# A graph network on one core: an addition moved between stages, and the order of GpSimd's and VectorE's work inside a layer-0 tile

## The chip, the cores and the metric

The kernel runs on one core of one Trainium2 chip. The metric is device time in microseconds, lower is better. A core has four engines that compute: TensorE (PE in the profile; its weight loads, which overlap the matmuls, are listed as PEld), VectorE (DVE), ScalarE (ACT) and GpSimd (POOL). SyncE (SP) issues most of the transfers. Each engine runs its own instructions in the order in which they were written for it, and waits on semaphores for the other engines. Operands lie in SBUF, 128 partitions wide; TensorE writes its sums to PSUM, and the other engines fetch them from there ("evict" them).

## The reference, cut to what matters

`x` is (8, 2048, 64): B = 8 samples, N = 2048 nodes, C = 64 features. `adj` is a 2048 x 2048 matrix whose rows are 0/1 patterns divided by their sums. Each of two layers applies `adj` twice, mixes the results by weights, adds the layer's input and normalizes over the features.

```python
def _L0_gnn_ref(x, A, embedding, weight, bias):
    w = jnp.einsum('nd,dkio->nkio', embedding, weight)     # one weight matrix per node, D = 16
    b = jnp.einsum('nd,do->no', embedding, bias)
    As = [jnp.eye(N, dtype=x.dtype), A]
    As.append(2.0 * (A @ As[-1]) - As[-2])                 # K = 3
    x_g = jnp.einsum('knm,bmc->bnkc', jnp.stack(As, 0), x)
    return jnp.einsum('bnki,nkio->bno', x_g, w) + b

# layer 1: x_stack = [x0] + 2 x [A x0, 2 A (A x0) - x0], then
    out = jnp.einsum('bnf,fo->bno', x_cat, weight) + bias

x = _layernorm(x + _L0_gnn_ref(x, adj, L0_gnn_embedding, L0_gnn_weight, L0_gnn_bias), axis=-1)
x = _layernorm(x + _L1_gnn_ref(x, adj, adj, L1_gnn_weight, L1_gnn_bias), axis=-1)
```

## The kernel before

The 2048 nodes are 16 tiles (NT) of 128 (P). Numbers of fp32 are split in a high and a low half (in layer 0 also a mixed one), so that TensorE can multiply them in the fp32r form; the splitting is most of the work of VectorE and ScalarE. The row factor 1/sum is kept apart from the 0/1 pattern. The stages, one after the other, with their stretches of the span in us:

- 10 to 123: the first hop, `adj` times x (L254).
- 123 to 226: the second hop as seven products of quarter matrices (`seven_products`, L631).
- 226 to 543: layer 0's mixing with the per-node weights, tile by tile (`mix0`, L415), with its normalization.
- 543 to 651: layer 1's first product with `adj`, called the third hop here, again `seven_products`, now with `to=to_zT`.
- 651 to 776: the fourth hop, the last normalization and the stores.

**A tile of layer 0.** TensorE multiplies the tile's operands `tt[k][n]` (k = x itself, its first and its second hop; n = high, low, mixed) by the 16 weight matrices of the embedding, in 8 slots (g, dg): g is a half of the samples, dg a group of 4 of the 16 matrices. Each slot fills one pair of PSUM banks from a pool of four pairs, `pm`, used in turn and by the transposes and projections of the same tile as well. In slots with dg > 0 VectorE takes the four parts of `pm` times the node's embedding value, and adds them into `acc` (L427). In the two slots with dg = 0 ScalarE scales them into `aside` (L425), GpSimd sums these (L430) and adds them to `acc`: for g = 0 ahead of slot (1, 2), for g = 1 at the tile's end (`add_aside`, L399).

The order of the work is written by hand: `ordered` keeps the written order on each engine, and the dictionary `at` says what is put into which slot, ahead of that slot's matmuls and evictions. During tile t there are put in:

- the operands of tile t + 1 (`parts`, L309 to 320). Each of the three generators `of_x`, `of_hop`, `of_second` has two steps: first ScalarE's copy to the high half (L312), then VectorE's low half (L314), ScalarE's scaled copy (L318) and GpSimd's sum of both (L319). `of_hop` takes its source from PSUM, where TensorE transposed it (buffer `pt`).
- the normalization of tile t - 1 (`layernorm`, L358 to 374), as a generator of steps. Ahead of the first step: VectorE's sum s (L361, L362) and GpSimd's subtraction xc (L364), written at the end of tile t - 1. First step: ScalarE's square (L352). Second: VectorE's sum ss (L369), ln_v (L333), ScalarE's root (L335). Third: VectorE's reciprocal and refinement (L338 to 344), GpSimd's product (L373). Before the change they stand in slots (0, 1), (0, 2) and (0, 3).
- GpSimd's product of tile t + 2's second hop with the row factors (`times_r`, L679 to 682), in slot (1, 2), and GpSimd's start of tile t + 1's sum, x plus the node's bias (`begin_sum`, L382 to 391, two instructions), in slot (1, 3).
- the normalized tile's transpose to `hT`, and after the tile the `project`ion of tile t - 1 by layer 1's weights (L434 to 454): for each g, TensorE fills `pu`, ScalarE copies two thirds of it to their places (L451), VectorE copies the last third and adds layer 1's bias `bias1` to it (L452). This third goes to bc(2, t), that is, the part that neither of layer 1's hops is applied to.

`bias1` is the last 64 columns of the tile `pack_sb`, which one transfer loads with the embedding values. That transfer, and those of `bias_sb`, `wl` and `rrow`, stand in the list `loads`, and are issued by SP's queue one at a time: the first in the later part of the first hop, while more than three are left (L507), the others one per step of the second hop (L621). `bias1`'s mean is taken off in `weights` (L184 to 187).

**The third hop.** `run` (L265) goes through the steps (p, kk) of seven products of KK = 8 steps. Each step makes its operands some steps ahead (`y_high` 4, `y_low` 3, `operands` 2) and then issues 8 matmuls in `use`; what stands in the dictionary `more` under (p, kk) is issued right after these. The output of the finished products is taken off PSUM by `put` on VectorE, through `todo`, two entries per step.

Of the kernel before, what the change touches and what calls it, by code (L numbers as in the profile page):

```python
# [9 lines left out]
F32 = mybir.dt.float32  # L10
# [4 lines left out]
ALU = mybir.AluOpType  # L15
# [3 lines left out]
P = 128  # L19
# [20 lines left out]
def pattern(  # L40
# [55 lines left out]
    def bc(s, t):  # L96
        return z[s][t].rearrange("p (b c) -> p b c", c=C)
# [9 lines left out]
    part = keep.tile([P, B], F32, tag="part", name="part")  # L107
    rrow = rowpool.tile([P, N], F32, tag="rrow", name="rrow")
    ident = keep.tile([P, P], F32, tag="ident", name="ident")
    pack_sb = const.tile([P, NT * D + C], F32, tag="pack", name="pack_sb")  # L110
    emb_sb = pack_sb[:, : NT * D].rearrange("p (t d) -> p t d", d=D)
    bias1 = pack_sb[:, NT * D :]
    ebias = const.tile([P, NT, C], F32, tag="ebias", name="ebias")


# [11 lines left out]
    def ordered(ins):  # L127
        if in_order:
            tc.keep_in_program_order(ins)
# [32 lines left out]
    wl = work2.tile([P, 5, C], F32, tag="t0", name="wl")  # L162
    bias_sb = work2.tile([P, N // 4 + C], F32, tag="t0", name="bias_sb")

    loads = [(bias_sb, bias), (pack_sb, pack[:, : NT * D + C]), (wl.rearrange("p k o -> p (k o)"), pack[:, NT * D + C :])]
    loads += [(rrow, diag.to_broadcast([P, N]))]

    def weights():

# [264 lines left out]
    def project(t, hT, pus=None):  # L434


        for g in range(2):
            pm = bank("pu") if pus is None else pus[g]
            for i in range(2):
                for j in range(2):  # L440
                    q = slice(j * C, (j + 1) * C)
                    nc.tensor.matmul(
                        pm[:, j, i * 3 * C : (i + 1) * 3 * C], lhsT=hT[q, 2 * g + i, :], rhs=v[q],
                        start=True, stop=True,
                    )
            got = pm[:, :, : 6 * C].rearrange("p j (i k c) -> p j i k c", i=2, k=3)

            order = ["p (i j) c -> p j i c", "p (j i) c -> p j i c", "p (j i) c -> p j i c"]
            to = [bc(k, t)[:, 4 * g : 4 * g + 4, :].rearrange(order[k], j=2) for k in range(3)]
            for k in range(2):  # L450
                ordered(nc.scalar.copy(to[k], got[:, :, :, 2 - k, :]))  # L451
            ordered(nc.vector.tensor_tensor(  # L452
                to[2], got[:, :, :, 0, :], bias1.unsqueeze(1).unsqueeze(1).to_broadcast([P, 2, 2, C]), ALU.add,
            ))


    HALF = N // 2
# [26 lines left out]
    def hop_x(g, kk, j):  # L484
        k = kk + KK * j

        def features(got):
            if g == 0 and k == 0:
                got["raws"] = [load_slab(adj[h, 0, :, :Q], [P, Q]) for h in range(2)]

        def operands(got):
            if g == 0 and k == 0:

                s = got["s"] = spool.tile([P, 2, Q], F32R, tag="s", name="s")
                hl = got["hl"] = [hpool.tile([P, B * C], F32R, tag="hl", name="hl") for _ in range(2)]
                high(z[0][0], hl)
                for h in range(2):
                    ordered(nc.vector.tensor_scalar(s[:, h], got["raws"][h], 0.0, None, ALU.not_equal))
                    if h == 0:
                        low(z[0][0], hl)  # L500
            else:
                if g == 0:
                    load(nc.sync, z[0][k], x[k].rearrange("n b c -> n (b c)"))
                raw = load_slab(adj[:, k, :, g * Q : (g + 1) * Q].rearrange("h m n -> m h n"), [P, 2, Q])
                got["s"] = places(raw)
                got["hl"] = halves(z[0][k])
                if g == 1 and len(loads) > 3:  # L507
                    load(nc.sync, *loads.pop(0))
            couple.append(got["s"])
            if j == 1:  # L510
                put_together(g, kk, *couple)
                couple.clear()

        def out(i):
            t = 4 * g + i if i < 4 else 4 * g + i + 4
            a, r = accs[i], rcol[:, t : t + 1]
            if i % 2:
                ordered(nc.vector.tensor_scalar_mul(z[1][t], a, r))
            else:
                ordered(nc.scalar.activation(z[1][t], a, AF.Copy, scale=r))  # L520

        def use(got):
            s, hl = got["s"], got["hl"]
            if kk == 0 and j == 0:
                accs[:] = banks(8)
            last = kk == KK - 1 and j == 1
            add_block(accs, s.rearrange("p h n -> p (h n)"), hl, kk == 0 and j == 0, last)
            if last:
                for i in range(8 if g == 0 else 4):
                    out(i)  # L530
            seen = xcpool.tile([P, 2, Q], BF16, tag="ln_xc", name="seen")
            i = g * NT + k
            ordered(nc.scalar.activation(seen, s, AF.Copy, accum_out=nonzero[:, i : i + 1]))
            if j == 1:
                ordered(nc.scalar.dma_start(out=quarters[kk, :, :, g, :], in_=seen))
            else:
                ordered(nc.scalar.dma_start(out=corner[kk, :, g, :], in_=seen[:, 0]))
            if last and g == 1:
                stores.pop(0)()

                todo.extend(lambda i=i: out(i) for i in range(4, 8))

        return [(4, features), (2, operands), (0, use)]


# [244 lines left out]
    def quarter_back(a, b, which):  # L790
        ts, got = range(8 * a, 8 * a + 8), []

        def two(n):
            for m in (n, n + 1):
                add_back(ts[m], got[m], b)

        work_here = [nothing, nothing, lambda: got.extend(back(ts, sums3[which], b)), nothing]
        return work_here + [lambda n=n: two(n) for n in range(0, 8, 2)]

    third = seven_products(0, to_zT, sums3, {  # L800
        (0, 5): [last_transposed],
        (0, 6): [last_projected],
        3: quarter_back(1, 1, 1), 4: quarter_back(0, 1, 0), 5: quarter_back(0, 0, 1),
    }, wait=2)

# [11 lines left out]
    for t in range(NT):  # L817
# [3 lines left out]
        if not last:  # L821
            got["tt"], of_x, of_hop, of_second = operands(t + 1)
            of_hop = of_hop()
            at[0, 2] += [lambda it=of_hop: next(it), lambda it=of_hop: next(it)]
            at[0, 3] += [lambda it=of_x: next(it)]
            at[1, 0] += [lambda it=of_x: next(it)]
            at[1, 1] += [lambda it=of_second: next(it)]
            at[1, 2] += [lambda it=of_second: next(it)]
            if t + 2 < NT:
                at[1, 2] += [lambda: times_r(t + 2)]  # L830
            at[1, 3] += [lambda: got.update(acc=begin_sum(t + 1))]
        if t > 0:
            at[0, 1] += [lambda: next(norm)]
            at[0, 2] += [lambda: next(norm)]
            at[0, 3].insert(0, lambda: next(norm))
            at[1, 2 if last else 3] += [lambda: got.update(hT=transpose(h, "hT"))]
        if last:
            at[0, 1] += [lambda: early(0)]
# [491 lines left out]
```

## Time and profile before

| what | us |
|---|---|
| median of 3 runs (lowest, highest) | 778.22 (777.99, 778.36) |
| the profiled execution's own time | 778.42 |
| its span | 776.6 |

The span runs from the first to the last recorded instruction of that execution, so 1.8 us of its time lie around it. Busy time by stage (us):

| stretch of the span | length | PE | DVE | ACT | POOL |
|---|---|---|---|---|---|
| first hop, 10 to 123 | 113.0 | 113.0 | 86.2 | 57.9 | 0 |
| second hop, 123 to 226 | 103.0 | 103.0 | 72.5 | 72.9 | 4.4 |
| layer 0, 226 to 543 | 317.0 | 310.7 | 274.3 | 147.3 | 217.1 |
| third hop, products 0 and 1, 543 to 573 | 30.0 | 30.0 | 20.0 | 24.6 | 2.9 |
| third hop, products 2 and 3, 573 to 603 | 30.0 | 30.0 | 17.2 | 22.7 | 0 |
| third hop, the rest, 603 to 651 | 48.0 | 48.0 | 29.7 | 32.2 | 0 |
| fourth hop, 651 to 776 | 125.0 | 119.0 | 82.6 | 19.8 | 24.8 |

The granted TensorE clock was 0.998 of full speed over the span. A tile of layer 0 takes about 19.8 us.

How to read the lines shown below. A line of the engine shares has the busy time of an engine, its share of the span and its number of instructions. A line of the waits view reads: engine, what it was about to write and its line in the code, the releaser it waited for, then us in total, times, longest. A line of a timeline has the start in us, the duration (of a run of several, from the first's start to the last's end), the engine, the line, the operation, out<-in with partitions x elements, and in brackets how long the engine had waited for what. "L427" is line 427 of the kernel.

### The profile page before, as it was taken

The numbers are of one execution on the slowest core, as the hardware profiler recorded it, in microseconds if no ns is written. First come the engines' busy times: TensorE is split into PE (matmuls) and PEld (weight loads), VectorE is DVE, ScalarE is ACT, GpSimd is POOL, SyncE is SP. The second block draws the span as 40 slices with busy tenths as digits, with TensorE's granted clock in tenths as the row PEclk, the third lists the DMA queues.
The fourth block names the chain that finished last, engine by engine and source line by source line (L and its number), as shares of the span: only waits on it lengthen the run. The fifth ranks groups of instructions, "written<-read, shape, count | busy, mean of one in ns | idle before, by whom it ended". The sixth has DMA issues, their size and how long they took to land.

```text
span 776.6 us, 17970 instructions
## 1 busy us (share of the span) xinstructions
PE 762.1 (98%) x7246; PEld 675.4 (87%) x7246; DVE 585.3 (75%) x1246; ACT 380.4 (49%) x720; POOL 249.9 (32%) x245
## 2 busy tenths in 40 slices
PE   9999999999999999999999999999999999999996
PEld 6888888888889999999999999999888888888885
DVE  6779766678648888888888888888765657768653
ACT  4446443878753444444444444445787664112111
POOL 0000000000036777777777777774100000012341
PEclk9999999999999999999999999999999999999999
DMA  8998995545410000000000000001444344565631
GB/s 309 384 383 294 335 322 173 188 156 170 163 42 16 17 16 16 15 16 16 16 16 16 16 15 16 2 29 43 142 158 148 137 149 144 170 189 158 215 130 45
DMA packets 73403, 96.77 MB, mean 125 GB/s; under 512 B 4704, under 2 KB 48224, under 8 KB 73184
## 3 DMA queue, kind: packets, MB, share of 16 engines
q1 hardware_dynamic: 61904, 76.66, 30.4%
q10 hardware_dynamic: 11408, 18.89, 6.5%
q8 instruction: 59, 0.97, 0.5%
q14 instruction: 32, 0.26, 0.1%
HBM read 76.65 MB, written 18.87 MB: 123 GB/s over the span
## 4 chain that ended last, share of the span: by engine, by line
PE 60%; DVE 25%; POOL 6%; issue 5%; ACT 2%; DMA 1%; SPq 0%; DVEq 0%; POOLq 0%
PE accT L631 26%; DVE acc L427 16%; PE acc L254 15%; PE a L254 9%; PE accT L254 6%; DVE parts L314 3%; PE pm L415 2%; POOL xc L364 2%; POOL acc L399 2%; DVE ln_v L333 2%; DVE s L361 1%; POOL acc L386 1%; DVE ss L369 1%; ACT sq L352 1%; DMA raw<-in_adj 1%
## 5 line engine op out<-in xcount | busy, mean ns | idle before, releaser
L415 PE MATMUL pm<-wh,hl 64*128 64x256 f32 x1536 | 239.9, 286 | 5.5 <-DVE acc L427 5.5
L415 PE MATMUL pm<-wm,parts 64*128 64x256 f32 x1536 | 235.0, 280 | 0.0
L415 PE MATMUL pm<-wl,parts 64*128 64x256 f32 x1536 | 234.9, 280 | 0.0
L631 PE MATMUL accT<-s,hl 128*128 128x512 f32 x896 | 205.7, 390 | 0.0
L631 PEld LDWEIGHTS accT<-s,hl 128*128 128x128 f32 x896 | 167.5, 188 | 35.4 <-issue 0.2
L427 DVE SCALAR_TENSOR_TENSOR acc<-pm,pack_sb,acc 128x256 f32<-128x256 f32 x384 | 185.1, 482 | 15.7 <-PE pm L415 3.8
L415 PEld LDWEIGHTS pm<-wh,hl 64*128 64x128 f32 x1536 | 164.4, 188 | 10.2 <-DVE acc L427 9.2
L415 PEld LDWEIGHTS pm<-wl,parts 64*128 64x128 f32 x1536 | 164.4, 188 | 0.0
L415 PEld LDWEIGHTS pm<-wm,parts 64*128 64x128 f32 x1536 | 164.2, 187 | 0.0
L619 ACT CAST s<-raw 128x1024 fp32r<-128x1024 bf16 x104 | 109.2, 1050 | 39.7 <-ACT hl L234 25.4
L254 PE MATMUL acc<-hl,s 128*128 128x512 f32 x512 | 117.5, 391 | 0.3 <-DVE s L223 0.2
L254 PEld LDWEIGHTS acc<-hl,s 128*128 128x128 f32 x512 | 95.7, 188 | 21.7 <-DVE hl L238 0.7
L682 POOL TENSOR_TENSOR z<-z,rrow 128x512 f32<-128x512 f32 x16 | 21.0, 1314 | 212.9 <-DVE z L655 212.9
L425 ACT ACTIVATE aside<-pm,pack_sb 128x256 f32<-128x256 f32 x128 | 50.2, 475 | 66.0 <-PE pm L415 66.0
L234 ACT CAST hl<-z 128x256 fp32r<-128x256 f32 (+1 forms) x96 | 47.5, 511 | 65.6 <-PE acc L254 24.9
L430 POOL TENSOR_TENSOR aside<-aside 128x512 f32<-128x512 f32 x64 | 69.7, 1090 | 14.8 <-ACT aside L425 12.2
L254 PE MATMUL a<-hl,s 128*128 128x512 f32 (+1 forms) x352 | 73.4, 370 | 0.0
L254 PEld LDWEIGHTS a<-hl,s 128*128 128x128 f32 x352 | 61.9, 188 | 11.3
L319 POOL TENSOR_TENSOR parts<-parts 128x512 fp32r<-128x512 f32 x45 | 57.8, 1285 | 27.8 <-DVE parts L314 27.1
L238 DVE TENSOR_TENSOR hl<-z,hl 128x512 fp32r<-128x512 f32 (+1 forms) x96 | 53.3, 563 | 16.2 <-ACT hl L234 13.5
L287 POOL TENSOR_TENSOR z<-z,got 128x512 f32<-128x512 f32 x3 | 4.8, 1625 | 143.4 <-ACT got L286 143.4
L254 PE MATMUL accT<-hl,s 128*128 128x512 f32 x192 | 44.3, 390 | 0.0
(130 smaller groups left out, 815.3 us busy)
## 6 DMA issues: line engine op xcount, KB each, us to landing
raw<-in_adj SPq DMA_DIRECT2D x59, 512.0 KB, 5.8
raw<-sums_of SPq DMA_DIRECT2D x64, 256.0 KB, 2.7
sums_of<-z ACTq DMA_DIRECT2D x16, 512.0 KB, 5.9
raw<-quarters SPq DMA_DIRECT2D x32, 256.0 KB, 2.7
raw<-in_adj SPq DMA_DIRECT2D x16, 384.0 KB, 3.0
quarters<-seen ACTq DMA_DIRECT2D x16, 256.0 KB, 5.8
xt<-in_xT SPq DMA_DIRECT2D x16, 256.0 KB, 2.6
z<-in_x SPq DMA_DIRECT2D x15, 256.0 KB, 6.8
```

The costliest lines, as they stand in the source:

```text
L234: ordered(nc.scalar.copy(to[0], src))
L238: ordered(nc.vector.tensor_tensor(to[1], src, to[0], ALU.subtract))
L254: nc.tensor.matmul(accs[i], lhsT=s[:, i * P : (i + 1) * P], rhs=hl[h], start=(first and h == 0), stop=(last and h == 1),)
L314: ordered(nc.vector.tensor_tensor(view(low), src, view(high), ALU.subtract))
L319: ordered(nc.gpsimd.tensor_tensor(mixed, mixed, low, ALU.add))
L415: nc.tensor.matmul(pm[:, j, i], lhsT=tt[k][n][q, 2 * g + i, :], rhs=w_parts[n][k][q, ds, :], start=(k == 0 and n == 0), stop=(k == 2 and n ...
L425: ordered(nc.scalar.activation(aside[g][:, d], got, AF.Copy, scale=e))
L427: ordered(nc.vector.scalar_tensor_tensor(part, got, e, part, ALU.mult, ALU.add))
L430: ordered(nc.gpsimd.tensor_tensor(aside[g][:, :n], aside[g][:, :n], aside[g][:, n : 2 * n], ALU.add))
L619: ordered(nc.scalar.copy(s, got["raw"]))
L631: nc.tensor.matmul(acc[i][:, c], lhsT=hl[h][:, i * P : (i + 1) * P], rhs=S[:, c * 512 : (c + 1) * 512], start=(kk == 0 and h == 0), stop=( ...
L682: ordered(nc.gpsimd.tensor_tensor(to, to, r, ALU.mult))
```

## The change

There are three parts.

1. `bias1` becomes a tile of its own with a transfer of its own (one entry more in `loads`, and the bound in L507 goes from 3 to 4). `project` copies all three thirds on ScalarE, without the bias. The bias is added later by a new function `add_bias(t)`, one VectorE instruction of 128x512 per tile, in the steps of products 2 and 3 of the third hop.
2. `times_r(t + 2)` moves from slot (1, 2) to slot (0, 2), and `begin_sum(t + 1)` from slot (1, 3) to slot (0, 3) (behind the normalization's product L373 and the high half of x).
3. For all tiles but the last, the normalization's square (L352) is written in slot (0, 2) between the high half of the hop and its low half, where before it stood a slot earlier, ahead of both. In the last tile, which prepares no next one, the second and third steps of the normalization move one slot forward, to (0, 1) and (0, 2).

```diff
--- before.py
+++ after.py
@@ -107,9 +107,9 @@
     part = keep.tile([P, B], F32, tag="part", name="part")
     rrow = rowpool.tile([P, N], F32, tag="rrow", name="rrow")
     ident = keep.tile([P, P], F32, tag="ident", name="ident")
-    pack_sb = const.tile([P, NT * D + C], F32, tag="pack", name="pack_sb")
+    pack_sb = const.tile([P, NT * D], F32, tag="pack", name="pack_sb")
     emb_sb = pack_sb[:, : NT * D].rearrange("p (t d) -> p t d", d=D)
-    bias1 = pack_sb[:, NT * D :]
+    bias1 = keep.tile([P, C], F32, tag="bias1", name="bias1")
     ebias = const.tile([P, NT, C], F32, tag="ebias", name="ebias")
 
 
@@ -162,8 +162,8 @@
     wl = work2.tile([P, 5, C], F32, tag="t0", name="wl")
     bias_sb = work2.tile([P, N // 4 + C], F32, tag="t0", name="bias_sb")
 
-    loads = [(bias_sb, bias), (pack_sb, pack[:, : NT * D + C]), (wl.rearrange("p k o -> p (k o)"), pack[:, NT * D + C :])]
-    loads += [(rrow, diag.to_broadcast([P, N]))]
+    loads = [(bias_sb, bias), (pack_sb, pack[:, : NT * D]), (wl.rearrange("p k o -> p (k o)"), pack[:, NT * D + C :])]
+    loads += [(bias1, pack[:, NT * D : NT * D + C]), (rrow, diag.to_broadcast([P, N]))]
 
     def weights():
 
@@ -447,11 +447,12 @@
 
             order = ["p (i j) c -> p j i c", "p (j i) c -> p j i c", "p (j i) c -> p j i c"]
             to = [bc(k, t)[:, 4 * g : 4 * g + 4, :].rearrange(order[k], j=2) for k in range(3)]
-            for k in range(2):
+            for k in range(3):
                 ordered(nc.scalar.copy(to[k], got[:, :, :, 2 - k, :]))
-            ordered(nc.vector.tensor_tensor(
-                to[2], got[:, :, :, 0, :], bias1.unsqueeze(1).unsqueeze(1).to_broadcast([P, 2, 2, C]), ALU.add,
-            ))
+
+    def add_bias(t):
+        to = bc(2, t)
+        ordered(nc.vector.tensor_tensor(to, to, bias1.unsqueeze(1).to_broadcast([P, B, C]), ALU.add))
 
 
     HALF = N // 2
@@ -504,7 +505,7 @@
                 raw = load_slab(adj[:, k, :, g * Q : (g + 1) * Q].rearrange("h m n -> m h n"), [P, 2, Q])
                 got["s"] = places(raw)
                 got["hl"] = halves(z[0][k])
-                if g == 1 and len(loads) > 3:
+                if g == 1 and len(loads) > 4:
                     load(nc.sync, *loads.pop(0))
             couple.append(got["s"])
             if j == 1:
@@ -800,6 +801,7 @@
     third = seven_products(0, to_zT, sums3, {
         (0, 5): [last_transposed],
         (0, 6): [last_projected],
+        **{(2 + t // KK, t % KK): [lambda t=t: add_bias(t)] for t in range(NT)},
         3: quarter_back(1, 1, 1), 4: quarter_back(0, 1, 0), 5: quarter_back(0, 0, 1),
     }, wait=2)
 
@@ -821,18 +823,18 @@
         if not last:
             got["tt"], of_x, of_hop, of_second = operands(t + 1)
             of_hop = of_hop()
-            at[0, 2] += [lambda it=of_hop: next(it), lambda it=of_hop: next(it)]
-            at[0, 3] += [lambda it=of_x: next(it)]
+            at[0, 2] += [lambda it=of_hop: next(it), lambda: next(norm) if t else None, lambda it=of_hop: next(it)]
+            if t + 2 < NT:
+                at[0, 2] += [lambda: times_r(t + 2)]
+            at[0, 3] += [lambda it=of_x: next(it), lambda: got.update(acc=begin_sum(t + 1))]
             at[1, 0] += [lambda it=of_x: next(it)]
             at[1, 1] += [lambda it=of_second: next(it)]
             at[1, 2] += [lambda it=of_second: next(it)]
-            if t + 2 < NT:
-                at[1, 2] += [lambda: times_r(t + 2)]
-            at[1, 3] += [lambda: got.update(acc=begin_sum(t + 1))]
         if t > 0:
-            at[0, 1] += [lambda: next(norm)]
-            at[0, 2] += [lambda: next(norm)]
-            at[0, 3].insert(0, lambda: next(norm))
+            if last:
+                at[0, 1] += [lambda: next(norm)]
+            at[0, 1 if last else 2] += [lambda: next(norm)]
+            at[0, 2 if last else 3].insert(0, lambda: next(norm))
             at[1, 2 if last else 3] += [lambda: got.update(hT=transpose(h, "hT"))]
         if last:
             at[0, 1] += [lambda: early(0)]
```

## The prediction

> **What bounds the kernel now.** I read the page's engine shares first, then layer 0 in stretches of one node tile, then who waited for whom there, then the timelines of VectorE and GpSimd over one tile.
>
> ```profile
> PE 762.1 (98%) x7246; PEld 675.4 (87%) x7246; DVE 585.3 (75%) x1246; ACT 380.4 (49%) x720; POOL 249.9 (32%) x245
> ```
>
> TensorE is busy 98% of the span, so all that can be won without touching its matmuls lies in its few gaps. In layer 0 (226 to 545 us) the waits view has these:
>
> ```profile
> DVE s L361 <- POOL acc L399: 16.2, 15, 1.2
> ...
> PEld pm L415 <- DVE acc L427: 9.2, 14, 1.1
> DVE parts L314 <- ACT hl L312: 5.7, 14, 0.4
> ```
>
> Once per tile, fourteen times, TensorE's weight load for the first bank of the next tile waits about 0.6 us for VectorE's evictions L427: it needs the PSUM bank of slot (1, 2). 9.2 us is the most that layer 0 can give. A tile takes this long (columns: stretch, length, then busy time of PE, PEld, DVE, ACT, POOL):
>
> ```profile
> 304.13:323.93 19.80, 19.49 (x320) 19.19 (x320) 17.33 (x37) 9.32 (x23) 14.21 (x15) 1.00 0.05 15
> ```
>
> No engine but TensorE is full, so the order on VectorE and GpSimd decides. The tile that starts at 304.13, VectorE's timeline and then GpSimd's:
>
> ```profile
> 308.84 2.04 DVE L427 SCALAR_TENSOR_TENSOR acc<-pm,pack_sb,acc 128x256 f32<-128x256 f32 x4
> 311.28 0.69 DVE L314 TENSOR_TENSOR parts<-pt,hl 128x512 fp32r<-128x512 f32 x1 [0.40 <-ACT hl L312]
> ...
> 312.60 0.86 DVE L333 SCALAR_TENSOR_TENSOR ln_v<-ss,eps 128x8 f32<-128x8 f32 x1
> 313.38 2.03 DVE L427 SCALAR_TENSOR_TENSOR acc<-pm,pack_sb,acc 128x256 f32<-128x256 f32 x4
> ...
> 315.95 0.17 DVE L344 SCALAR_TENSOR_TENSOR ln_r<-ln_q,ln_r 128x8 f32<-128x8 f32 x1
> ...
> 317.99 0.68 DVE L314 TENSOR_TENSOR parts<-xt,hl 128x512 fp32r<-128x512 f32 x1
> 318.59 2.04 DVE L427 SCALAR_TENSOR_TENSOR acc<-pm,pack_sb,acc 128x256 f32<-128x256 f32 x4
> 320.54 1.38 DVE L314 TENSOR_TENSOR parts<-z,hl 128x512 fp32r<-128x512 f32 x1
> ```
>
> ```profile
> 312.15 1.29 POOL L319 TENSOR_TENSOR parts<-parts 128x512 fp32r<-128x512 f32 x1
> 316.20 1.04 POOL L373 TENSOR_TENSOR xc<-xc,ln_r 128x512 f32<-128x512 f32 x1 [2.77 <-DVE ln_r L344]
> 318.84 1.29 POOL L319 TENSOR_TENSOR parts<-parts 128x512 fp32r<-128x512 f32 x1 [1.60 <-DVE parts L314]
> 320.09 2.43 POOL L430 TENSOR_TENSOR aside<-aside 128x512 f32<-128x512 f32 x2
> ```
>
> See two things. GpSimd has two holes, 2.77 and 1.60 us. And two VectorE instructions last 0.7 us too long: L333 takes 0.86, where L344 on the same 128x8 takes 0.17, and ends at 313.46, with GpSimd's L319 (313.44). L314 on z takes 1.38, where the same shape on xt takes 0.68; it ends at 321.93, 0.55 after GpSimd's first L430 (320.09 + 1.29, the page's mean). Both read two operands from SBUF. The evictions read one (the other is PSUM) and run beside GpSimd unhurt.
>
> **The Trainium skill.** "SBUF — State Buffer", section "Who interferes with whom", says that a VectorE instruction with two SBUF inputs contends with a GpSimd instruction that reads SBUF, that the later one blocks fully, and that issue order decides. The trace agrees (the 0.86 and 1.38 above). The same section says ScalarE never waits for such a port, which is why moving the bias operation to ScalarE adds no new conflict. "Perfetto Trace Analysis", "Optimizing Scalar/DVE Operations", warns that moving work between GpSimd and VectorE may not help because of that shared port; here it is moved within GpSimd, and the same caution applies.
>
> **The change, part by part.**
>
> Bias. Per tile two VectorE adds L452 (0.41 each, 0.74 together) go; ScalarE gets two copies more (0.37 each, like L451), between 324.3 and 325.1, before its next task at 326.40: nothing. Sixteen adds of 128x512 come in the third hop, one per step in products 2 and 3, 0.68 each (the L655 form), 10.9 us. There (573 to 603 us) VectorE was busy 17.2 of 30 us while TensorE never stopped, and the operands are made three steps, some 5.5 us, ahead: nothing; without that cover it would be the excess over 30 us, some 0 to 2 us. The split pack load and a 32 KB load more on SP's queue move the rrow load one step back, far ahead of its use at 214 us; TensorE does not wait in that stage: nothing.
>
> GpSimd's tail. L682 (1.31) and the L386 pair (1.47) leave the end of the tile, so L399 follows the last eviction at once and L361 starts about 1 us earlier. But the next thing on VectorE, the (0, 1) evictions at 308.84, needs TensorE's bank, whose last matmuls start at 308.50; ScalarE's L425 starts 0.32 after such a matmul. So they cannot start before about 308.82. The 1 us becomes idle time: gain 0 to 0.02.
>
> High half ahead of the square. L314 on pt no longer waits 0.40 for ScalarE: it starts when the evictions end, 310.80, and ends 311.49. GpSimd's L319 follows 0.17 later (as 318.84 follows 318.67): 311.66 to 312.95. L333, asking 1.32 after L314's start (312.12), is again held by it and ends 312.97, so VectorE is 0.49 earlier from here. L344 ends at 315.63.
>
> L682 in the first hole. From 312.91 to about 314.4, with L333 let in first. VectorE evicts PSUM meanwhile, and L373 starts only at 315.71: nothing.
>
> L386 behind L373. This decides. L373 runs 315.71 to 316.75, the pair follows at 316.71, its second at 317.41 (0.70 later, the pair takes 1.47) until 318.17. VectorE asks for L314 on xt at 317.99 - 0.49 = 317.50, two SBUF inputs, 0.09 after the second L386 has begun. Before, it met an idle GpSimd. Now it is held, and ends, like L314 on z, 0.55 after the holder: 318.72. Before it was 318.67. The 0.49 won is spent, with 0.05 on top. Everything after it hangs on that instruction as before: L319, L430, the held L314 on z, the (1, 2) evictions, TensorE.
>
> Who wins so close a call? Before has one nearly as close (GpSimd, then VectorE):
>
> ```profile
> 242.27 0.74 POOL L399 TENSOR_TENSOR acc<-acc,aside 128x256 f32<-128x256 f32 x1
> ```
>
> ```profile
> 242.31 1.25 DVE L314 TENSOR_TENSOR parts<-z,hl 128x512 fp32r<-128x512 f32 x1
> ```
>
> VectorE came 0.04 late and was held 0.57. One that already waits when GpSimd goes from one instruction to the next is let in, as at 214 us:
>
> ```profile
> 214.23 2.76 POOL L682 TENSOR_TENSOR z<-z,rrow 128x512 f32<-128x512 f32 x2 [212.93 <-DVE z L655]
> ```
>
> ```profile
> 214.94 0.88 DVE L238 TENSOR_TENSOR hl<-t,hl 128x256 fp32r<-128x256 f32 x1 [0.19 <-ACT hl L234]
> ```
>
> (0.88 instead of 0.42, yet ended before the pair did.) So L333 passes L682, and L314 loses to the second L386.
>
> Last tile. Its normalization is one slot earlier, so TensorE's 0.9 us wait for L373 at 536.4 goes; the next bank then waits for the (0, 3) evictions, which end some 0.4 earlier (two stalls of VectorE for ScalarE's square, 2.18 and 0.46, shrink to about 1.9 and 0.5, and L238 is less often held): -0.4, bounds -0.9 and 0. In tile 1, L333 and L319 nearly tie: 0 to +0.5 once; I take 0.
>
> **Sum.** Twelve or thirteen tiles at +0.03 (0.05 less the 0.02; bounds -0.03 and +0.05) make +0.4, the last tile -0.4: span 776.6. The profiled execution took 778.42 with a span of 776.6, so 1.8 lie around it and it stands 0.2 above the median 778.22. I forecast 778.3, no change.
>
> **Rivals.**
> (a) VectorE wins at L386. L314 on xt ends at 318.18, the second L386 at 318.79, L319 runs 318.75 to 320.04, L430 starts at 320.00, and L314 on z asks at 320.05: held again, ending 321.84 for 321.93, 0.09 less per tile, -1.2, 777.1. If it wins there too, GpSimd's last L319 of the tile slips to 324.6 (320.6 + 2.12 + 0.72 + 1.27 less overlaps), and the next tile's ninth pair of matmuls, 1.0 after its start, needs it: the start can move from 323.93 to about 323.7 only, 14 x -0.19 = -2.7, 775.6. For it: the margin is 0.09 us. Against: 242.31.
> (b) The whole stall goes: 778.3 - 9.2 = 769.1. For it: VectorE has 2.5 us of idle time per tile. Against: GpSimd's last L319, as in (a), is late then.
> (c) Slower: L682 follows L319 without a wait and takes the port ahead of the waiting L333. L333 is then held 1.29 more, VectorE stands 0.8 behind instead of 0.49 ahead, and L386 holds L314 on top: 0.05 + 1.29 = 1.3 per tile, x13 = +17, 795. It decides if GpSimd's next instruction is preferred to a waiting VectorE. Against: 214.94, and each held L314 on z slipped in between two L430.
>
> **How the numbers follow.** No change 0.70; (a) 0.16; (b) 0.05; (c) 0.04; another loss, as from the third hop's adds, 0.05. 0.2% is 1.6 us, about what a measurement of this kernel can tell from no change. (a) lies half on each side of it. The no-change case alone spans 777.4 to 779.4; with (a) and a small loss the range is 775.5 to 779.8. Faster 0.20, same 0.70, slower 0.10.
>
> **What would show it.** In the changed profile: L314 on pt without its 0.40 wait and L361 waiting less; L314 on xt near 1.2 us instead of 0.68, ending with the L386 pair; the wait of L415 for L427 still some 0.6 per tile. It is wrong if L314 on xt stays at 0.68, or if L333 exceeds 1 us.

## The result, and the profile after

The changed kernel took 777.60 us (median of 14 runs, 776.88 to 778.71) against 778.31 us for the kernel before (14 runs, 777.85 to 779.06): a ratio of 0.9990, 95% interval 0.9982 to 0.9998. That is 0.7 us faster: less than half of what the prediction took as the least change that can be told, but no change lies just outside the interval. The forecast was 778.3, no change. The profiled execution took 777.52 us, with a span of 775.6. In the changed kernel line numbers from 455 on are one or two higher: L631 of the kernel before is L632 there, L682 is L683.

The engine shares of the changed kernel, as first shown of the kernel before:

```profile
PE 761.5 (98%) x7246; PEld 675.2 (87%) x7246; DVE 590.7 (76%) x1230; ACT 386.5 (50%) x752; POOL 251.1 (32%) x245
```

VectorE has 5.4 us more and 16 instructions fewer (32 small adds gone, 16 larger ones come), ScalarE 6.1 us more. TensorE's gaps are the question again. The waits in layer 0:

```profile
DVE s L361 <- POOL acc L399: 14.9, 16, 1.2
DVE acc L427 <- PE pm L415: 14.2, 16, 2.2
...
PEld pm L415 <- DVE acc L427: 8.8, 14, 0.7
PE pm L415 <- DVE acc L427: 5.9, 15, 1.3
```

TensorE still waits fourteen times for VectorE's evictions at the tile boundary, 8.8 us instead of 9.2. VectorE's wait for ScalarE at L314 is gone from the list, and VectorE now waits 14.2 us for TensorE where it waited 3.8: the time that GpSimd's shorter tail gives it ahead of slot (0, 1) is idle (0.80 us in a tile). So VectorE did win time, and TensorE did not get it. Where it went is seen in all tiles at once, if the instructions of L314 are listed by their source, between 260 and 520 us (minimum, median and maximum in ns). First the kernel before:

```profile
L314 DVE TENSOR_TENSOR parts<-pt,hl x13: 690/691/693, 271.6 to 509.6; 128x512 fp32r<-128x512 f32 x13
L314 DVE TENSOR_TENSOR parts<-xt,hl x13: 680/681/682, 278.4 to 516.3; 128x512 fp32r<-128x512 f32 x13
...
  ACT hl L312: 5.3, 13
```

and the changed one:

```profile
L314 DVE TENSOR_TENSOR parts<-pt,hl x13: 680/680/681, 270.2 to 508.1; 128x512 fp32r<-128x512 f32 x13
L314 DVE TENSOR_TENSOR parts<-xt,hl x13: 1216/1219/1230, 276.9 to 514.8; 128x512 fp32r<-128x512 f32 x13
```

The wait for ScalarE (5.3 us, 0.41 each) is gone, and the same VectorE instruction on xt takes 1219 ns instead of 681, in each of the 13 tiles, with hardly any spread. GpSimd's timeline in one tile shows what stands beside it, then VectorE's:

```profile
314.76 1.05 POOL L373 TENSOR_TENSOR xc<-xc,ln_r 128x512 f32<-128x512 f32 x1 [1.51 <-DVE ln_r L344]
315.76 1.47 POOL L386 TENSOR_TENSOR acc<-z,ebias 128x256 f32<-128x256 f32 x2
```

```profile
316.55 1.23 DVE L314 TENSOR_TENSOR parts<-xt,hl 128x512 fp32r<-128x512 f32 x1
317.70 2.03 DVE L427 SCALAR_TENSOR_TENSOR acc<-pm,pack_sb,acc 128x256 f32<-128x256 f32 x4
```

The second L386 starts at about 316.49 (0.73 into the pair, half of 1.47), the L314 on xt at 316.55, 0.06 later, and ends at 317.78, 0.55 after the pair. This is the hold that the prediction computed (0.09 late, end 0.55 after the holder). The other one that it computed, L333 held as before, is there too (0.86 in the kernel before):

```profile
311.17 0.84 DVE L333 SCALAR_TENSOR_TENSOR ln_v<-ss,eps 128x8 f32<-128x8 f32 x1
```

Where, then, do 0.7 us come from? The starts of TensorE's matmuls cut the span into stretches; the table takes them from its timeline in both profiles, one execution each (the start, the first matmul of the second hop (L631), the first L415, the first L415 of the third tile and of the last, the first L631 of the third hop, the last matmul, the end).

| stretch, us | before | after | difference |
|---|---|---|---|
| start to the second hop | 123.18 | 122.69 | -0.49 |
| second hop | 103.55 | 103.55 | 0 |
| layer 0, first and second tile | 37.75 | 37.31 | -0.44 |
| layer 0, the 13 tiles after them | 257.74 | 257.76 | +0.02 |
| layer 0, last tile | 20.88 | 20.60 | -0.28 |
| third and fourth hop | 226.59 | 226.61 | +0.02 |
| last matmul to the end | 6.95 | 7.13 | +0.18 |

The first row scatters: it lay from 122.63 to 123.31 in the kernels with the changed kernel's loads, and from 123.01 to 123.20 in the four with those of before. The rows of the first two tiles and of the last repeat within 0.05 us in runs where nothing that bears on them differs, the row of the 13 tiles within 0.2. The second tile and the last one give -0.72 together, the thirteen in between nothing that can be told. The first row and the last come from single executions; that the loads add one or two tenths to the difference of the medians is not excluded.

### The profile page after: what moved, and what is told of

It reads as the page before. It is cut to its first block, busy times and chain, and to the rows that moved or that the text cites. A ratio compares the mean times of both kernels' runs of the same rounds, so it can differ in the third digit from the quotient of the medians.

```text
span 775.6 us, 17992 instructions
## 1 busy us (share of the span) xinstructions
PE 761.5 (98%) x7246; PEld 675.2 (87%) x7246; DVE 590.7 (76%) x1230; ACT 386.5 (50%) x752; POOL 251.1 (32%) x245
## 4 chain that ended last, share of the span: by engine, by line
PE 69%; DVE 26%; issue 4%; POOL 0%; ACT 0%; DVEq 0%; POOLq 0%
PE accT L632 26%; DVE acc L427 18%; PE acc L254 15%; PE pm L415 10%; PE a L254 9%; PE accT L254 6%; DVE parts L314 3%; DVE ln_v L333 2%; DVE ss L369 1%; PE accT L782 1%; PE first L143 1%; DVE ln_q L341 0%; DVE ln_q L342 0%; DVE ln_r L344 0%; DVE ln_r L338 0%
## 5 line engine op out<-in xcount | busy, mean ns | idle before, releaser
L415 PE MATMUL pm<-wh,hl 64*128 64x256 f32 x1536 | 240.9, 286 | 5.9 <-DVE acc L427 5.9
L415 PE MATMUL pm<-wm,parts 64*128 64x256 f32 x1536 | 235.9, 280 | 0.0
L415 PE MATMUL pm<-wl,parts 64*128 64x256 f32 x1536 | 235.9, 280 | 0.0
L632 PE MATMUL accT<-s,hl 128*128 128x512 f32 x896 | 205.7, 390 | 0.0
L427 DVE SCALAR_TENSOR_TENSOR acc<-pm,pack_sb,acc 128x256 f32<-128x256 f32 x384 | 185.1, 482 | 26.3 <-PE pm L415 14.2
L632 PEld LDWEIGHTS accT<-s,hl 128*128 128x128 f32 x896 | 167.5, 188 | 35.4 <-issue 0.2
L415 PEld LDWEIGHTS pm<-wh,hl 64*128 64x128 f32 x1536 | 165.2, 188 | 10.6 <-DVE acc L427 8.8
L415 PEld LDWEIGHTS pm<-wl,parts 64*128 64x128 f32 x1536 | 165.2, 187 | 0.0
L415 PEld LDWEIGHTS pm<-wm,parts 64*128 64x128 f32 x1536 | 165.0, 187 | 0.0
L683 POOL TENSOR_TENSOR z<-z,rrow 128x512 f32<-128x512 f32 x16 | 21.0, 1318 | 212.4 <-DVE z L656 212.4
L430 POOL TENSOR_TENSOR aside<-aside 128x512 f32<-128x512 f32 x64 | 69.8, 1090 | 16.2 <-ACT aside L425 13.7
L319 POOL TENSOR_TENSOR parts<-parts 128x512 fp32r<-128x512 f32 x45 | 58.0, 1289 | 16.6 <-DVE parts L314 16.0
```

Of the source, the lines that this page charges most:

```text
L319: ordered(nc.gpsimd.tensor_tensor(mixed, mixed, low, ALU.add))
L415: nc.tensor.matmul(pm[:, j, i], lhsT=tt[k][n][q, 2 * g + i, :], rhs=w_parts[n][k][q, ds, :], start=(k == 0 and n == 0), stop=(k == 2 and n ...
L427: ordered(nc.vector.scalar_tensor_tensor(part, got, e, part, ALU.mult, ALU.add))
L430: ordered(nc.gpsimd.tensor_tensor(aside[g][:, :n], aside[g][:, :n], aside[g][:, n : 2 * n], ALU.add))
L632: nc.tensor.matmul(acc[i][:, c], lhsT=hl[h][:, i * P : (i + 1) * P], rhs=S[:, c * 512 : (c + 1) * 512], start=(kk == 0 and h == 0), stop=( ...
L683: ordered(nc.gpsimd.tensor_tensor(to, to, r, ALU.mult))
```

## The experiments

Each kernel was timed beside the kernel before. "Two tiles" (the first and the second), "13 tiles" and "last tile" are the rows of the table above.

| run | us | ratio to before, 95% interval | two tiles | 13 tiles | last tile |
|---|---|---|---|---|---|
| before | 778.31 | | 37.75 | 257.74 | 20.88 |
| after | 777.60 | 0.9990 (0.9982 to 0.9998) | 37.31 | 257.76 | 20.60 |
| bias_only | 778.23 | 0.9999 (0.9991 to 1.0008) | 37.77 | 257.86 | 20.88 |
| square_first | 778.53 | 1.0004 (0.9995 to 1.0012) | 38.30 | 257.81 | 20.60 |
| begin_sum_back | 769.96 | 0.9895 (0.9880 to 0.9911) | 36.78 | 250.74 | 20.59 |
| high_first_only | 770.06 | 0.9896 (0.9880 to 0.9911) | 36.69 | 250.72 | 20.89 |
| last_as_before | 778.08 | 0.9995 (0.9987 to 1.0004) | 37.30 | 257.81 | 20.87 |
| lnv_one_input | 777.38 | 0.9987 (0.9979 to 0.9995) | 37.32 | 257.64 | 20.61 |
| before_lnv | 778.36 | 1.0002 (0.9993 to 1.0010) | 37.76 | 257.70 | 20.88 |
| begin_sum_in_hole | 775.69 | 0.9969 (0.9957 to 0.9981) | 37.79 | 255.70 | 20.62 |
| lnv_on_act | 768.60 | 0.9877 (0.9861 to 0.9894) | 37.28 | 248.93 | 20.60 |
| before_lnv_act | 768.31 | 0.9868 (0.9851 to 0.9884) | 36.87 | 248.94 | 20.32 |
| best | 769.17 | 0.9880 (0.9864 to 0.9897) | 36.77 | 250.78 | 19.70 |
| best2 | 767.98 | 0.9867 (0.9851 to 0.9884) | 36.75 | 248.92 | 20.33 |

### The bias alone

The kernel before, with the bias part of the change and nothing else.

```diff
-            for k in range(2):
+            for k in range(3):
                 ordered(nc.scalar.copy(to[k], got[:, :, :, 2 - k, :]))
-            ordered(nc.vector.tensor_tensor(
...
+    def add_bias(t):
+        to = bc(2, t)
+        ordered(nc.vector.tensor_tensor(to, to, bias1.unsqueeze(1).to_broadcast([P, B, C]), ALU.add))
```

> The kernel before with the bias part of the change alone. Theory A (the whole change is small because two things inside a layer-0 tile cancel, and what is left of it, 0.7 us, comes from layer 0's second tile and from its last tile): the bias part is worth nothing, 778.3 +- 0.3; the tile boundaries keep their 0.66 us, the second tile's its 1.09, and the third hop shows no gap of TensorE in products 2 and 3. Theory B (the bias part is where the 0.7 us come from, since VectorE loses 0.74 us per tile at the boundary): 777.6. Theory C (the sixteen adds cost something in the third hop, and the rest of the change gains more than is seen): 779 to 780.

Measured: 778.23, no difference, and the three rows of layer 0 stay as before. The interval reaches from -0.7 to +0.6 us, so the median alone would not rule out that the 0.7 us come from the bias; the rows of layer 0 do for that stage. TensorE was busy for all of the changed kernel's third-hop stretch, although VectorE now works 26.4 of its 30 us, where it worked 17.2:

```profile
573.00:603.00 30.00, 30.00 (x134) 24.86 (x133) 26.39 (x60) 22.31 (x34) 0.00 (x0) 1.00 0.48 149
```

(Columns: stretch, length, busy time of PE, PEld, DVE, ACT, POOL, then clock, DMA share, GB/s.) So the bias costs nothing and gives nothing that is seen here.

### begin_sum back at the tile's end

```diff
-            at[0, 3] += [lambda it=of_x: next(it), lambda: got.update(acc=begin_sum(t + 1))]
+            at[0, 3] += [lambda it=of_x: next(it)]
             at[1, 0] += [lambda it=of_x: next(it)]
             at[1, 1] += [lambda it=of_second: next(it)]
             at[1, 2] += [lambda it=of_second: next(it)]
+            at[1, 3] += [lambda: got.update(acc=begin_sum(t + 1))]
```

> The kernel after with begin_sum back in slot (1, 3) and nothing else changed. Theory A (a tile is bound by VectorE's chain, and the second begin_sum instruction takes back what was won by holding L314 on xt): L314 on xt falls from 1.23 to 0.68 us, the wait at each tile boundary shrinks from 0.66 to 0.1 or 0.2, 13 or 14 tiles x 0.5 = 6.5 to 7.5 us less, 770 to 771.5. Rival D (what bounds a tile is elsewhere, in TensorE's or ScalarE's own order, and 19.83 us per tile stay whatever VectorE saves): 777.6. Rival E (GpSimd's tail, longer by 1.5 us again, delays L399 and the norm's first sum, and takes a part): 774 to 776.

Measured: 769.96, 1.0% faster than the kernel before, 7.6 us faster than the kernel after. Its VectorE timeline at the same place, then GpSimd's:

```profile
315.31 0.69 DVE L314 TENSOR_TENSOR parts<-xt,hl 128x512 fp32r<-128x512 f32 x1
```

```profile
313.51 1.04 POOL L373 TENSOR_TENSOR xc<-xc,ln_r 128x512 f32<-128x512 f32 x1 [1.51 <-DVE ln_r L344]
316.16 1.29 POOL L319 TENSOR_TENSOR parts<-parts 128x512 fp32r<-128x512 f32 x1 [1.60 <-DVE parts L314]
```

With GpSimd idle from 314.55 on, L314 on xt takes 0.69 again, 0.54 less than in the kernel after, and the 13 tiles fall by 7.02 us, 0.54 each. GpSimd's longer tail at the tile's end costs nothing that shows: TensorE's wait for L427 at the tile boundaries is gone from the list. So the place of begin_sum is what made the change small; it was worth 7.6 us.

### Which part of the change takes ScalarE's wait away

The prediction gave the whole 0.49 us to the high half's place ahead of the square. Two runs separate it from GpSimd's moves. `square_first` is the kernel after with the square ahead again:

```diff
-            at[0, 2] += [lambda it=of_hop: next(it), lambda: next(norm) if t else None, lambda it=of_hop: next(it)]
+            at[0, 2] += [lambda it=of_hop: next(it), lambda it=of_hop: next(it)]
...
-            if last:
-                at[0, 1] += [lambda: next(norm)]
+            at[0, 1] += [lambda: next(norm)]
```

> The kernel after with the square written ahead of the hop's high half again, in slot (0, 1), in all tiles; the bias and GpSimd's moves stay. The prediction held that the high half's place ahead of the square wins 0.49 us per tile. If that is so, VectorE is 0.49 later and still meets the second begin_sum instruction: L314 on pt waits 0.4 again, and the time is 777.6 + 13 x 0.49 = 784. Rival: GpSimd's moves alone already bring xc (L364) 0.9 us earlier in the tile, so that the square is over before the high half is wanted (square 308.3 to 308.9, high half to 309.5, evictions until 309.9): no wait at L314 on pt from the third tile on, only the second tile gives its 0.44 back: 778.0.

`high_first_only` is the kernel before with this one edit of the change:

```diff
-            at[0, 2] += [lambda it=of_hop: next(it), lambda it=of_hop: next(it)]
+            at[0, 2] += [lambda it=of_hop: next(it), lambda: next(norm) if t else None, lambda it=of_hop: next(it)]
...
-            at[0, 1] += [lambda: next(norm)]
+            if last:
+                at[0, 1] += [lambda: next(norm)]
```

> The kernel before with one edit: the square written behind the high half of the hop, in slot (0, 2), for all tiles but the last; bias, times_r and begin_sum as before. Theory A: L314 on pt loses its 0.40 us wait, nothing holds L314 on xt (0.68 us), so each tile is 0.45 to 0.5 us shorter: 778.3 - 13 x 0.48 = 772. Rival D (a tile's 19.83 us do not hang on VectorE): 778.3. Rival F (the last parts L319 on z come too late for the next tile's ninth pair of matmuls, as in rival (a) of the prediction): 775.6.

Measured: `square_first` 778.53, 0.9 above the kernel after, all of it in the two first tiles (38.30 for 37.31); the 13 tiles stay at 257.81, and L314 on pt waits for ScalarE once, 0.41 us, in the second tile:

```profile
DVE parts L314 <- ACT hl L312: 0.4, 1, 0.4
```

The prediction's reading, which asked for 784, is refuted: with GpSimd's tail shortened, xc comes early enough for the square to be over in time, from the third tile on. And `high_first_only` gives 770.06: the order of the high half does the same without GpSimd's moves. Either is enough, and the change makes both. Which of GpSimd's two moves does it was not separated. In the second tile, where 0.44 was expected and 0.99 measured, `square_first` has both costs at once: the wait for ScalarE is back, and begin_sum still holds L314 on xt (1.22 us at 258.52). The kernel before had only the first of them (37.75), `begin_sum_back` neither (36.78).

So one move of the change, that of the square in `high_first_only`, alone gives 8.2 us on the kernel before.

### The last tile

```diff
-            at[0, 1 if last else 2] += [lambda: next(norm)]
-            at[0, 2 if last else 3].insert(0, lambda: next(norm))
+            at[0, 2] += [lambda: next(norm)]
+            at[0, 3].insert(0, lambda: next(norm))
```

> The kernel after with the last tile's normalization steps back in slots (0, 2) and (0, 3). Theory A: what the change gained is 0.44 us in layer 0's second tile and 0.28 us in its last. Then the last tile, from its boundary to the third hop's first matmul, goes from 20.60 back to 20.88 us, everything else stays as in the kernel after, and the time is 777.9. Rival: the shorter last tile comes from the bias or from GpSimd's moves, and stays at 20.60.

Measured: 778.08, and the last tile's row goes back to 20.87 with all else unchanged. The median moves by 0.48, more than these 0.27, which is within what such medians scatter by; the row is the better measure. TensorE's waits around the last tile, in the kernel before (those of `last_as_before` read the same), then in the kernel after:

```profile
PE pt L300 <- POOL xc L373: 0.9, 1, 0.9
PE pm L415 <- DVE acc L427: 0.7, 2, 0.4
```

```profile
PE pm L415 <- DVE acc L427: 1.6, 2, 1.3
```

The wait for L373 did go, as said, and the wait for the evictions that follows it grew from 0.4 to 1.3: most of the gain was spent one step later. These are the evictions of slot (0, 3). Counted from the tile's first L415 they ended at 14.86 us in the kernel before (537.08 - 522.22) and at 14.65 in the kernel after (535.96 - 521.31), 0.21 earlier where the prediction had 0.4. One step more of VectorE's was in their way: the earlier place put L333 beside GpSimd's L430 (VectorE's line of the kernel before, then VectorE's and GpSimd's of the kernel after):

```profile
531.41 0.17 DVE L333 SCALAR_TENSOR_TENSOR ln_v<-ss,eps 128x8 f32<-128x8 f32 x1
```

```profile
527.81 0.68 DVE L333 SCALAR_TENSOR_TENSOR ln_v<-ss,eps 128x8 f32<-128x8 f32 x1
```

```profile
526.35 2.12 POOL L430 TENSOR_TENSOR aside<-aside 128x512 f32<-128x512 f32 x2
```

That this hold is what kept the gain small is not shown: with L333 on ScalarE (`lnv_on_act`, below) the last tile's row stays at 20.60.

### begin_sum in the remaining hole

GpSimd has a hole of 1.51 us ahead of L373 in the kernel after, about the length of the pair of L386. This run puts begin_sum there.

```diff
-            at[0, 3] += [lambda it=of_x: next(it), lambda: got.update(acc=begin_sum(t + 1))]
+            at[0, 3] += [lambda it=of_x: next(it)]
+            at[0, 2] += [lambda: got.update(acc=begin_sum(t + 1))]
```

> The kernel after with begin_sum in slot (0, 2), behind times_r and ahead of L373, in GpSimd's remaining hole of 1.51 us. Theory A prices it: L338 is free, L341 meets the second begin_sum instruction, waits for its end and takes 0.55 instead of 0.17 us, so L344 and L373 come 0.40 later; L314 on xt then meets an idle GpSimd and takes 0.68 instead of 1.23. Net -0.15 us per tile, x13 = -2.0: 775.5, with the boundary's wait at some 0.5 us. Rivals: L373 is then the bound and costs more than it gains (778 or above); or the VectorE instruction is let in between the two, and the full 0.54 comes (770.5).

Measured: 775.69; the 13 tiles take 257.76 - 255.70 = 2.06 us less than the kernel after. The second tile loses 0.48 again (37.79 for 37.31). The VectorE lines of a later tile:

```profile
314.57 0.57 DVE L341 SCALAR_TENSOR_TENSOR ln_q<-ln_r 128x8 f32<-128x8 f32 x1
...
317.41 0.68 DVE L314 TENSOR_TENSOR parts<-xt,hl 128x512 fp32r<-128x512 f32 x1
```

The hold has moved from the large L314 to the small L341 (0.57 for 0.17), and is smaller by 0.15 per tile. A hole of GpSimd that is as long as the work was not free here: what counted was which VectorE instructions fell into it.

### The other held instruction, L333

If VectorE's chain sets the tile, then taking away the hold of L333 (0.84 us instead of 0.17) should do as much as taking away that of L314. Two runs tried a form with one operand from SBUF, on the kernel after and on the kernel before:

```diff
-        ordered(nc.vector.scalar_tensor_tensor(va, ss, 1.0 / C, eps.to_broadcast(list(ss.shape)), ALU.mult, ALU.add))
+        ordered(nc.vector.tensor_scalar(va, ss, 1.0 / C, EPS, ALU.mult, ALU.add))
```

> The kernel after with ln_v (L333) computed with the two constants as immediates, so that it reads one operand from SBUF instead of two (the same values). Theory A (a tile of layer 0 is bound by VectorE's chain, and this chain loses time only where a two-input instruction is held by GpSimd): L333 falls from 0.84 to 0.17 us, L314 on xt is held as before since L373 and L386 move with it, and each tile is shorter by 0.54 us, where TensorE has no gap left (19.29 per tile, as in the two runs before); the second tile stays at 37.3 from layer 0's first matmul, since L333 was not held there. 777.6 - 13 x 0.54 = 770.6. Rival: the hold of L333 is no more than a small instruction's own time, or hides behind the evictions: 777.6.

> The kernel before with the same one edit to L333 and nothing of the change. Theory A: L333 from 0.86 to 0.17 us in every tile, the 0.40 us wait of L314 on pt stays, and the boundary's 0.66 us go as well: 13 x 0.54 = 7.0, and up to 1.0 in the second tile: 770.2 to 771.2. If the boundary is set by L314's wait for ScalarE in some way that VectorE's 0.69 us cannot shorten: 778.3.

Measured: 777.38 and 778.36, nothing gained in either. Their lines, after and before:

```profile
311.27 0.84 DVE L333 TENSOR_SCALAR ln_v<-ss 128x8 f32<-128x8 f32 x1
```

```profile
312.52 0.87 DVE L333 TENSOR_SCALAR ln_v<-ss 128x8 f32<-128x8 f32 x1
```

The expectation fell at its first step: the form with one operand is held just as long. The Trainium skill ("SBUF — State Buffer", "Who interferes with whom") says that `tensor_scalar` can, when its operands meet certain conditions, enter a mode that takes both port pairs, and then contends with GpSimd too; the 0.84 us agree with that, though no run here tells which mode it was in. So these two runs did not test the question. The next two move the instruction to ScalarE:

```diff
-        ordered(nc.vector.scalar_tensor_tensor(va, ss, 1.0 / C, eps.to_broadcast(list(ss.shape)), ALU.mult, ALU.add))
+        ordered(nc.scalar.activation(va, ss, AF.Identity, bias=eps, scale=1.0 / C))
```

> The kernel after with ln_v (L333) computed by ScalarE instead of VectorE, ahead of the root (the same values). The last try left the instruction on VectorE in a form with one operand, and it was held for the same 0.84 us, so the hold itself was not taken away. Theory A: on ScalarE nothing holds it, VectorE's chain loses 0.77 us per tile, L314 on xt is still held behind begin_sum, and the tile falls to TensorE's 19.29: 777.6 - 13 x 0.54 = 770.6. Rival: VectorE is not what sets the tile, 777.6; or the longer ScalarE chain (root 0.2 to 0.3 us later, high half of xt too) takes the gain: 774 to 777.

> The same one edit to the kernel before, with nothing of the change. Theory A: the 0.86 us of L333 go, the 0.40 us wait of L314 on pt stays, the boundary's 0.66 us go: 13 x 0.54 = 7.0, and about 0.9 in the second tile: 770.3. Rival as above: 778.3, or 775 to 778.

Measured: 768.60 and 768.31. L314 on xt is still held in the first of them:

```profile
314.23 1.21 DVE L314 TENSOR_TENSOR parts<-xt,hl 128x512 fp32r<-128x512 f32 x1
```

and yet the 13 tiles take 248.93 us, 8.8 us less than in the kernel after. Theory A holds, and its floor was wrong: 19.15 us per tile (248.93 / 13), not the 19.29 of `begin_sum_back`. The kernel before with this edit takes nearly the same, 248.94; its expectation kept the 0.40 us wait of L314 on pt, but only three of the fourteen waits are left, 1.1 us in all. Both times are about 2 us lower than the expectation, of which 13 x 0.14 = 1.8 is this floor.

### A version that beats both

`best` is `begin_sum_back` with another order in the last tile: the third hop's first operands ahead of the square, the sum behind slot (0, 1)'s evictions. `best2` adds ln_v on ScalarE.

```diff
             if last:
-                at[0, 1] += [lambda: next(norm)]
-            at[0, 1 if last else 2] += [lambda: next(norm)]
-            at[0, 2 if last else 3].insert(0, lambda: next(norm))
+                at[0, 1] += [lambda: early(0), lambda: next(norm)]
+            at[0, 2] += [lambda: next(norm)]
+            at[0, 3].insert(0, lambda: next(norm))
...
-            at[0, 1] += [lambda: early(0)]
```

> The kernel after with begin_sum back in slot (1, 3), and in the last tile the third hop's first operands written ahead of the norm's square, the sum ss behind the evictions of slot (0, 1), L373 in slot (0, 3). VectorE then evicts slot (0, 1) while it waited 1.9 us for the square; TensorE's 1.3 us in the last tile shrink to some 0.3: last tile 19.5 to 20.0 instead of 20.6, 769.0 to 769.4 against 769.96 with begin_sum alone. If L373 then comes too late for the transposes as in the kernel before: 770.2.

> The last version (begin_sum back in slot (1, 3), the last tile's new order) with ln_v on ScalarE. If 19.15 us per tile, as with ln_v on ScalarE in both kernels, are TensorE's own time and the earlier 19.29 were still VectorE's, then 13 x 0.14 = 1.8 us go: 767.4, with the last tile at 19.7. If the two savings on VectorE do not add beyond 19.29 here: 769.2.

Measured: 769.17, with a last tile of 19.70 instead of 20.59; then 767.98, where the 13 tiles fell to 248.92. With L314 on xt free as well as L333 they take no less than with L333 alone, and three kernels with different orders on VectorE and GpSimd end at 248.92 to 248.94: this is where VectorE no longer sets the tile. TensorE's starts agree. From the last L415 of one tile to the first of the next (the projection's matmuls lie between) it took about 1.91 us in the 13 tiles of the kernel after, 1.38 in those of `begin_sum_back` and 1.26 in those of these three. That TensorE's own work is what remains is the likely reading; no run made that work shorter. The last tile went back to 20.33, so the two edits do not add there; its profile has TensorE waiting for L373 again (0.3 us) and for evictions (0.4), and the cause was not tried. 767.98 is the fastest kernel of the study, 1.3% below the kernel before, and not told apart from `before_lnv_act`, whose interval is nearly the same.

## Why the prediction was right or wrong

- **What bounds a tile, and the hold at begin_sum: right.** VectorE at the boundary, the 0.49 us spent on L314 on xt behind the second L386, L333 let in ahead of L683: all as written. `begin_sum_back` showed the cause by taking it away. The size was a little off: +0.03 for each of twelve or thirteen tiles made +0.4 in the sum, and the 13 together gave +0.02. Rival (c) did not happen: L333 took 0.84, not over 1. Rival (a) gave 777.1, near to the measured time, and was not what happened either, since VectorE lost at L386 in all 13 tiles. Rival (b), the whole stall gone at 769.1, is about what the change gives with begin_sum left where it was (769.96). Two limits of the text did not hold once the hold was gone. GpSimd's last L319, which was to let the next tile start no more than about 0.2 us earlier, did not bind: the 13 tiles became 0.54 us shorter each in `begin_sum_back` and 0.68 in `best2`. And "9.2 us is the most that layer 0 can give" was too low: in `best2` layer 0 is 9.8 us shorter ahead of its last tile alone (36.75 + 248.92 against 37.75 + 257.74).
- **The second tile: wrong, and this is the step that failed.** It is tile 1 of the text, which said "In tile 1, L333 and L319 nearly tie: 0 to +0.5 once; I take 0". It was -0.44. The line of the kernel before, then two of the changed kernel, a close race that VectorE won:

```profile
253.14 0.86 DVE L333 SCALAR_TENSOR_TENSOR ln_v<-ss,eps 128x8 f32<-128x8 f32 x1
```

```profile
252.16 0.17 DVE L333 SCALAR_TENSOR_TENSOR ln_v<-ss,eps 128x8 f32<-128x8 f32 x1
```

```profile
252.20 1.30 POOL L319 TENSOR_TENSOR parts<-parts 128x512 fp32r<-128x512 f32 x1
```

L333 started 0.04 us ahead of L319 and took 0.17; in the kernel before it started at 253.14, into a running L319, and took 0.86. Beside the 0.49 us of every tile, that takes 0.69 more off VectorE's chain; the hold at L386 (1.22 at 257.06) gives 0.54 back, and 0.2 is lost at L341, held to 0.36 by L683: 0.49 + 0.69 - 0.54 - 0.2 = 0.44. In the later tiles of the changed kernel GpSimd starts this L319 after a wait for VectorE's L314, ahead of L333; in this one it follows GpSimd's own L430 without a wait, and L333 is there first. The prediction also had in hand that the boundary after this tile was the worst of the fourteen (the longest wait was 1.1 us where the others were about 0.66), and treated all fourteen alike: there was 0.4 us more to win there than in any other tile. Taking the tie as a loss, or nothing, left out the gain of the only one of the equally treated tiles in which gain and loss do not cancel. The other side of the tie was never priced.
- **The last tile: right in sign, mis-sized.** -0.4 was forecast, -0.28 measured: the evictions of slot (0, 3), for which TensorE waits next, ended 0.21 us earlier and not 0.4. The text did not price the 0.68 us that L333 takes there beside L430.
- **The sum.** Forecast +0.4 - 0.4 + 0 = 0; measured +0.02 - 0.28 - 0.44 = -0.70, against -0.71 by the medians. Two terms came out 0.4 us lower than forecast (the 13 tiles by 0.38, the second tile by 0.44), the last tile 0.12 higher. The text also took 1.6 us as the least that can be told from no change; the interval of the 14 runs is 0.6 us to either side, and so 0.7 could just be told.
- **High half ahead of the square: the sum right, the credit wrong.** "Gain 0 to 0.02" for GpSimd's tail and 0.49 for the high half was one of two ways to share a gain that each part makes alone, as `square_first` and `high_first_only` showed.
- **The bias at nothing: right** (`bias_only`).
- **Two operands from SBUF** as the reason why L333 is held was too narrow: with one it is held as well.

## What to carry to other kernels

When two engines share a port, look for the loss in an instruction's own duration; here it stood in no list of waits: list one line's durations over all tiles by source, and look for a second value. Before work is put into a queue's hole, look for instructions of the sharing engine that fall due in it and would be held; the place of begin_sum, slot (0, 3) or (1, 3), decided 7.6 us. Before pricing a change as a sum over equal tiles, take the tiles that are not equal (the first, the second, the last) one by one: here they held nearly all of the difference.

## What the runs showed of the hardware

- Who gets the port was decided by a few hundredths of a microsecond, in both cases by the recorded start: in the second tile L333, 0.04 us ahead of GpSimd's L319, took 0.17; L314 on xt, 0.06 behind the second L386, took 1.23, and it took 1.22 to 1.23 in each of the 13 tiles.
- Where both engines had work waiting they took turns (the first lines below are VectorE's, the second GpSimd's timeline there). In the second tile of `begin_sum_in_hole` L341, L342 and L344 follow one another beside GpSimd's L683 and the pair of L386, and take 0.37, 0.67 and 0.67 us instead of 0.17: each ends within 0.04 us of the GpSimd instruction that ran as it started (the first L386 taken as half of the pair), and the next one is held anew. The three lose 1.2 us together, more than twice what the large L314 on xt lost.

```profile
254.65 0.37 DVE L341 SCALAR_TENSOR_TENSOR ln_q<-ln_r 128x8 f32<-128x8 f32 x1
255.05 0.67 DVE L342 TENSOR_TENSOR ln_q<-ln_q,ln_v 128x8 f32<-128x8 f32 x1
255.76 0.67 DVE L344 SCALAR_TENSOR_TENSOR ln_r<-ln_q,ln_r 128x8 f32<-128x8 f32 x1
```

```profile
253.70 1.30 POOL L683 TENSOR_TENSOR z<-z,rrow 128x512 f32<-128x512 f32 x1
254.95 1.46 POOL L386 TENSOR_TENSOR acc<-z,ebias 128x256 f32<-128x256 f32 x2
```

- A `tensor_scalar` of 8 elements per partition, with one operand from SBUF, was held by GpSimd for 0.84 us like the form with two. A reciprocal of the same shape was not: in `begin_sum_in_hole` L338 took 0.19 us at 314.34, while the pair of L386 ran (313.65 to 315.11). So the number of operands alone did not tell whether an instruction is held.
